# Rows and one-hots of the messages in rings of sets of four, filled in turns of opposite order, and the experts' relu from last part to first

## The chip, the cores and the metric

The kernel runs on one core of a Trainium2 chip. The metric is the device time of one launch in microseconds (us). Before the change it was 1699.68 us, the median of 13 runs (1698.12 to 1706.53). The engines are named PE (matrix products), ACT (activations), DVE (vector operations), POOL (here almost only the issue of indirect DMAs) and SP (issue of the other DMAs). They run side by side and wait for one another by semaphores: each engine posts an increment when an instruction is done, if somebody needs it, and an instruction can wait for a value.

## The reference

One layer of a graph transformer over 6250 nodes of 256 features, with 100000 edges that are sorted by their target:

```
xn = layernorm(x)
h = xn @ W
deg = segment_sum(edge_weight, dst) + 1 ; dinv = rsqrt(deg)
agg = segment_sum(dinv[src]*edge_weight*dinv[dst] * h[src], dst) + dinv^2 * h
gnn = relu(0.5*(layernorm(agg + b)*gamma + beta) + 0.5*xn)
mix = linear attention over xn (8 heads, elu+1 features), projected
x   = x + gnn + mix
z   = layernorm(x)
w, e = softmax over, and places of, the 2 largest of 16 logits z @ gate_w + gate_b
moe = sum over the two experts e of w * (relu(z @ w1[e] + b1[e]) @ w2[e] + b2[e])
x   = x + layernorm(z + moe)*gamma + beta
```

Everything is float32. The edge sum, the gather of h[src] and the segment sum, is the part that the change bears on most; the expert's two products are the other.

## The kernel before

The nodes are held in 49 tiles of 128. The edges are cut into 782 chunks of 128 in the order of their targets. For each chunk, POOL gathers the 128 rows of `h` from memory into a tile `hrow` (line 1364, an indirect DMA of 128 KB), DVE builds a one-hot matrix `hot` of the targets, scaled by the edge weights (line 1369), and PE multiplies the two into a bank `acc` (line 1377; two instructions of 128x256 in the profile for one product). A group of eight chunks shares a bank; DVE then adds it to `agg` (line 1386).

The program is written out by slots, one for each chunk. In slot s stand the gather of chunk s, the one-hots that are due (a product's one-hot is built HOT = 4 slots ahead of it) and the products that are due: chunk c is multiplied in slot c + LAG, with LAG = 11, falling to LAST_LAG = 6 near the end. `hrow` is a pool of ROWS = 22 buffers and `hot` one of HOTS = 9, each taken in turn: gather c needs the place of chunk c - 22, so it waits until that chunk's product is done, and one-hot c waits for product c - 9.

Between these, a planner written out by hand, `Weave`, runs the rest of the layer: pieces are generators that yield the number of slots until their next step. `attend` (lines 573 on) makes keys, queries and their sums for a tile; `residual` (681) joins graph and attention parts; `route` (847) picks the experts; `scatter` (1022) writes the tokens to the experts' slots by indirect DMAs on POOL (line 1040); `expert` (1073) runs one block of 128 slots through an expert; `combine` (1168) gathers the two results of each token on POOL (line 1180) and makes the output. The order of instructions on PE, DVE, ACT and SP is the order in which they are written. 114 expert blocks are run, about one for every seven slots in the middle of the kernel.

`expert` first loads the weights and the tokens through SP, transposes the tokens on PE (`xtp`, copied by ACT), and multiplies by w1 into one bank `hp`, 8 products shown as 16 instructions. Then ACT makes the relu in four parts of 128 columns, f = 0 to 3 (line 1129), each into a part of `hT`, and PE multiplies the four parts by w2 into `yp` (line 1133), again in the order f = 0 to 3:

```
        for f in range(FJ):
            act(hT[:, f, :], hp[:, f, :], AF.Relu, bias=b1[:, f:f + 1], scale=1.0)
        yield apart - lag
        yp = bank("yp")
        for f in range(FJ):
            nc.tensor.matmul(yp[:, :D], hT[:, f, :], w2[:, f, :], start=(f == 0), stop=(f == FJ - 1 and not as_row))
```

After the last chunk, the pool of rows is closed and its room is used for the rows of the combine (`late_row`): NROW places, of which 12 hold shifted tokens ("more") and the others gathered results ("got").

Of the kernel before, what the change touches and what calls it, by code (L numbers as in the profile page):

```python
# [23 lines left out]
F32 = mybir.dt.float32  # L24
# [7 lines left out]
P = 128  # L32
N = 6250
D = 256
# [17 lines left out]
FJ = F // P  # L52
# [4 lines left out]
def rows(t):  # L57
    return min(P, N - t * P)
# [53 lines left out]
HB = 168  # L112
NB3 = 2 * D
QT = 36
ROWS = 22
LAG, LAST_LAG = 11, 6
HOT, HOTS = 4, 9

# [14 lines left out]
def group_of(c):  # L135

    return (c + CPR // 2) // CPR


def product_at(c):  # L140

    return c + max(LAST_LAG, min(LAG, LAST_LAG + (NCH - 30 - c) // 8))


def evicted_at(c):

    return product_at(c) + (3 if c < 16 * PHASES[-2] else 1)
# [111 lines left out]
def windowed_layer(ctx: ExitStack, tc: tile.TileContext, X, ident, loc_t, w_t, src_t, W, b, gamma, beta, wqT, wkvT, wprojT, bproj,  # L259
                   gate_w, gate_b, experts, f_gamma, f_beta, out):  # L260
    nc = tc.nc
# [135 lines left out]
    with tc.tile_pool(name="deg", bufs=1) as sp, \  # L397
# [59 lines left out]
        for n in (C // 2, C // 2, C, C, C):  # L457
# [8 lines left out]
            for c in range(c0, min(c0 + n, NCH)):  # L466
                g0 = 4 * group_of(c)
                h0 = g0
                while h0 < g0 + HI:
                    i = h0 // HB  # L470
# [34 lines left out]
        for i in range(3):  # L505
            v.tensor_reduce(deg16[:, i, :], deg[:, i, :3 * HB].rearrange("p (h s) -> p h s", s=3),
                            axis=AX.X, op=OP.add)
# [37 lines left out]
    mp = msg.enter_context(tc.tile_pool(name="w_msg", bufs=4))  # L545
# [3 lines left out]
    def bank(name):  # L549
        return ps.tile([P, 512], F32, name=name, tag="bank")  # L550
# [103 lines left out]
    def agg(t):  # L654
        return hTs[t // 2][:, t % 2 * D:(t % 2 + 1) * D] if t < 4 else ring[(t - 4) % RING]
# [411 lines left out]
    def sync(to, source):  # L1067
        issued[0] = nc.sync.dma_start(to, source).ins
        return issued[0]
# [3 lines left out]
    def expert(n, j, homes, bank, gap, apart, lag, as_row=False):  # L1073

        def row(i):
            if not loaded.get(i):
                _, regs = nc.values_load_multi_w_load_instructions(
                    s["rows"][0:1, i, j:min(j // 8 * 8 + 8, ends[j])], engines=[mybir.EngineType.SP],
                    min_val=0, max_val=(MOST if i == 0 else NE - 1) * P,
                    skip_runtime_bounds_check_because="bounded by a minimum where it is computed")  # L1080
                loaded[i] = list(regs)
            return loaded[i].pop(0)

        at, slots = row(1), row(0)
        w1p = homes["w1"].take()
        w1 = w1p()
        sync(w1, experts[bass.ds(at, P), :WA])
        w1 = w1.rearrange("p (c f) -> p c f", c=2)
        xp = homes["x"].take()
        xs = xp()  # L1090
        i = sync(xs, xslots[bass.ds(slots, P), :])
        if n is not None:
            for m in range(n + 1, len(PHASES)):
                tc.declare_no_dep(i, group=f"tokens_{m}", reason="a full block takes no more tokens")
            tc.add_to_no_dep_group("loads", i)
        yield gap[0]
        w2p = homes["w2"].take()
        w = w2p()[:, :WROW - WA]
        if as_row:
            sync(w[:, :WB - WA], experts[bass.ds(at, P), WA:WB])  # L1100
            b2 = w[:3, WB - WA:WB - WA + D // 2].bitcast(BF)
            sync(b2, b2rows[bass.ds(at, 3), :])
        else:
            sync(w, experts[bass.ds(at, P), WA:])
            b2 = w[:, WB - WA:]
        w2 = w[:, :FJ * D].rearrange("p (j d) -> p j d", j=FJ)
        b1 = w[:, FJ * D:FJ * D + FJ]
        yield gap[1]
        tp = bank("xtp").rearrange("p (k c) -> p k c", k=4)
        for c in range(2):  # L1110
            nc.tensor.transpose(tp[:, c, :], xs[:, c * P:(c + 1) * P], ident)
        homes["x"].give(xp)
        yield lag
        xTp = homes["xT"].take()
        xT = xTp().rearrange("p (k c) -> p k c", k=2)
        nc.scalar.copy(xT, tp[:, :2, :])  # L1116
        yield apart - lag

        hp = bank("hp").rearrange("p (f c) -> p f c", f=FJ)
        for f in range(FJ):  # L1120
            for c in range(2):
                nc.tensor.matmul(hp[:, f, :], w1[:, c, f * P:(f + 1) * P], xT[:, c, :], start=(c == 0), stop=(c == 1))  # L1122
        homes["xT"].give(xTp)
        homes["w1"].give(w1p)
        yield lag
        hTp = homes["hT"].take()
        hT = hTp().rearrange("p (k c) -> p k c", k=FJ)
        for f in range(FJ):
            act(hT[:, f, :], hp[:, f, :], AF.Relu, bias=b1[:, f:f + 1], scale=1.0)  # L1129
        yield apart - lag  # L1130
        yp = bank("yp")
        for f in range(FJ):
            nc.tensor.matmul(yp[:, :D], hT[:, f, :], w2[:, f, :], start=(f == 0), stop=(f == FJ - 1 and not as_row))  # L1133
        if as_row:
            nc.tensor.matmul(yp[:, :D], ones3, b2, start=False, stop=True)
        homes["hT"].give(hTp)
        yield lag
        y_ = homes["y"].take()
        y = y_()
        if as_row:  # L1140
            nc.scalar.copy(y, yp[:, :D])
        else:
            v.tensor_add(y, yp[:, :D], b2)
        homes["w2"].give(w2p)
        yield 1
        before_it = issued[0]
        i = sync(yslots[bass.ds(slots, P), :], y)
        if n is not None:
            tc.declare_no_dep(i, group="stores", reason="every block has rows of its own", keep=[before_it])
            tc.add_to_no_dep_group("stores", i)  # L1150
            stores[j] = i
            for m, (_, limit) in enumerate(LIMITS):
                if j >= limit:
                    tc.declare_no_dep(i, group=f"gathers_{m}", reason="later blocks hold no token of the first tiles")
                    tc.add_to_no_dep_group(f"late_{m}", i)
        homes["y"].give(y_)
# [85 lines left out]
    def spare(t, n=1):  # L1242
        return range(t, t + n), lambda: Q[:, t:t + n, :].rearrange("p t c -> p (t c)")

    NROW = ROWS
    ringed = ExitStack()
    rp = ringed.enter_context(tc.tile_pool(name="w_ring", bufs=1))
    late = []

    def late_row(i):  # L1250
        if not late:
            late.append(msg.enter_context(tc.tile_pool(name="w_late", bufs=1)).tile([P, NROW, D], F32, name="late"))
        return late[0][:, i, :]
# [11 lines left out]
             "more": Places(*[((), lambda i=i: late_row(i)) for i in range(LATE)], *[spare(t) for t in range(9, 13)]),  # L1265
             "got": Places(*[((), lambda i=i: late_row(i)) for i in range(LATE, NROW)],
                           *[((NT - 1,), lambda j=j: ring[j]) for j in range(RING)])}
# [82 lines left out]
    hrows, hots, accs = {}, {}, {}  # L1350
# [7 lines left out]
    while slot <= evicted_at(NCH - 1) or weave.steps:  # L1358
        for t in range(NT * (slot + PRE) // PRE, NT * (slot + PRE + 1) // PRE if slot < 0 else 0):
            table(t)  # L1360
        c = slot
        if 0 <= c < NCH:
            hrows[c] = rp.tile([P, D], F32, name="hrow", bufs=ROWS)
            nc.gpsimd.indirect_dma_start(  # L1364
                out=hrows[c], out_offset=None, in_=hs,
                in_offset=IndirectOffsetOnAxis(ap=src_t[:, c:c + 1], axis=0))
        for c in hot_at.get(slot, ()):
            hots[c] = mp.tile([P, P], F32, name="hot", bufs=HOTS)
            v.tensor_scalar(hots[c], iota_g[:, group_of(c) % 2, :], loc_t[:, c:c + 1], w_t[:, c:c + 1],  # L1369
                            op0=OP.is_equal, op1=OP.mult)  # L1370
        for c in sum_at.get(slot, ()):
            g = group_of(c)
            begin = c == 0 or group_of(c - 1) != g
            end = c == NCH - 1 or group_of(c + 1) != g
            if begin:
                accs[g] = aps.tile([P, D], F32, name="acc")
            nc.tensor.matmul(accs[g], hots.pop(c), hrows.pop(c), start=begin, stop=end)  # L1377
        for g in evict_at.get(slot, ()):
            acc = accs.pop(g)
            t = (g - 1) // 2  # L1380
            parts = [(t, 0, P)] if g % 2 else [(t, P // 2, P), (t + 1, 0, P // 2)]
            for t, p0, p1 in parts:
                p1 = min(p1, rows(t)) if 0 <= t < NT else 0
                if p1 > p0:
                    assert t in begun and t not in summed, (slot, t, summed_at)
                    v.scalar_tensor_tensor(agg(t)[p0:p1], acc[p0:p1, :], dinv[p0:p1, t:t + 1], agg(t)[p0:p1],  # L1386
                                           op0=OP.mult, op1=OP.add)
        weave.run(slot)
        slot += 1
        if slot == product_at(NCH - 1) + 1:  # L1390
            ringed.close()
# [4 lines left out]
    with tc.If(again[0]), ExitStack() as tail:  # L1396
        tail.enter_context(by_hand(tc))
        mp = tail.enter_context(tc.tile_pool(name="w_again", bufs=2))
# [516 lines left out]
```

## Time and profile before

| What | Value |
|---|---|
| median of 13 runs | 1699.68 us |
| the profiled execution's own time | 1703.65 us |
| its span | 1701.9 us |
| mean granted clock of PE | 0.876 |
| PE busy | 1307.5 us (77%) |
| POOL busy | 955.4 us (56%) |
| DVE busy | 913.4 us (54%) |
| ACT busy | 497.5 us (29%) |
| first gather to last gather | 107.7 to 1400.0 us |

The profile is one execution. A group of instructions is given by line, engine, operation and tile, `out<-in`, with the number of instructions, their busy time and the mean of one in ns, then the idle time that the engine had before them and what ended most of it. "issue" is idle time that ended with nothing that the profile can show; "remote" is a semaphore of another engine whose instruction is not identified. PE's ends are modelled from its starts.

### The profile page before, as it was taken

To read this page: it belongs to the slowest core of one execution; us is meant where nothing else is said; L and a number is where in the kernel's file an instruction comes from. 1 tells how busy PE (TensorE), PEld (TensorE's weight loads), DVE (VectorE), ACT (ScalarE), POOL (GpSimd) and SP (SyncE) were. 2 spreads that over 40 slices of the span, in tenths; PEclk is the share of its full clock that TensorE was granted. 3 is DMA by queue.
4 is the path that set the end of the run, shared out by engine and by line. 5 is a ranking of instruction groups with operands and counts; after the bars stand their busy time and mean duration, and the time that the engine had idled before them with its cause. 6 is when DMAs were issued, how large, how long until landed. Compare 5 with 4: busy or idle time off the path is not lost. (4 is left out here: it accounts for less than half of the span.)

```text
span 1701.9 us, 24398 instructions
## 1 busy us (share of the span) xinstructions
PE 1307.5 (77%) x6927; PEld 1035.0 (61%) x6927; DVE 913.4 (54%) x3303; ACT 497.5 (29%) x1428; POOL 955.4 (56%) x998
## 2 busy tenths in 40 slices
PE   4985988976846778878788787887987998958780
PEld 3853655655634657757566575775766776847660
DVE  7842333346956545644645545555464456626654
ACT  6442333322211122212222122221221132426663
POOL 1036666666666666666665666666666552155531
PEclk9997999988876889979889798998988998978995
DMA  8774555563334557657667565766767785779982
GB/s 271 238 256 136 189 184 164 185 205 95 93 105 142 176 191 235 225 192 232 229 195 256 177 220 191 254 230 193 230 221 235 252 261 179 274 244 312 363 292 72
DMA packets 180593, 357.20 MB, mean 210 GB/s; under 512 B 27157, under 2 KB 119692, under 8 KB 180442
## 3 DMA queue, kind: packets, MB, share of 16 engines
q1 hardware_dynamic: 110334, 204.18, 35.1%
q0 software_dynamic: 47712, 128.17, 24.5%
q10 hardware_dynamic: 22396, 23.10, 4.2%
q8 instruction: 61, 1.00, 0.2%
q14 instruction: 90, 0.74, 0.1%
HBM read 279.28 MB, written 76.06 MB: 209 GB/s over the span
## 5 line engine op out<-in xcount | busy, mean ns | idle before, releaser
L1364 POOL DMA_INDIRECT hrow<-w_hs,src_t x782 | 754.5, 965 | 521.2 <-issue 175.6
L1377 PE MATMUL acc<-hrow,hot 128*128 128x256 f32 x1564 | 452.0, 409 | 41.0 <-issue 25.2
L1377 PEld LDWEIGHTS acc<-hrow,hot 128*128 128x128 f32 x1564 | 294.1, 204 | 115.0 <-issue 64.3
L1369 DVE TENSOR_SCALAR hot<-iota_g,loc_t,w_t 128x128 f32<-128x128 f32 x782 | 245.6, 353 | 127.5 <-PE acc L1377 57.7
L1133 PE MATMUL yp<-early,hT 128*128 128x256 f32 x584 | 167.7, 438 | 57.9 <-issue 44.8
L1129 ACT ACTIVATE hT<-hp,early 128x128 f32<-128x128 f32 x292 | 83.1, 367 | 415.4 <-issue 227.5
L1133 PEld LDWEIGHTS yp<-early,hT 128*128 128x128 f32 x584 | 125.3, 222 | 91.0 <-issue 55.8
L1122 PE MATMUL hp<-Q,early 128*128 128x128 f32 x992 | 131.0, 286 | 11.3 <-ACT Q L1116 6.3
L1122 PEld LDWEIGHTS hp<-Q,early 128*128 128x128 f32 x992 | 127.2, 202 | 17.3 <-ACT Q L1116 7.5
L588 PE MATMUL kq<-early,xnT 128*128 128x512 f32 (+1 forms) x196 | 102.0, 646 | 22.0 <-ACT xnT L584 21.1
L1040 POOL DMA_INDIRECT w_xslots<-Q,slot_i x92 | 90.0, 978 | 45.5 <-issue 41.5
L1133 PE MATMUL yp<-Q,hT 128*128 128x256 f32 x328 | 94.6, 438 | 26.0 <-issue 18.1
L1122 PE MATMUL hp<-Q 128*128 128x128 f32 x832 | 107.5, 285 | 9.1 <-issue 7.5
L1122 PEld LDWEIGHTS hp<-Q 128*128 128x128 f32 x832 | 105.5, 201 | 12.8 <-issue 8.1
L1386 DVE SCALAR_TENSOR_TENSOR agg<-acc,dinv,agg 64x256 f32<-64x256 f32 x135 | 65.1, 482 | 75.7 <-remote 35.4
L749 PE MATMUL mix<-M,two_b 128*128 128x256 f32 (+1 forms) x196 | 66.2, 460 | 48.2 <-issue 31.3
L1133 PEld LDWEIGHTS yp<-Q,hT 128*128 128x128 f32 x328 | 70.1, 222 | 42.1 <-issue 21.2
L1129 ACT ACTIVATE hT<-hp,Q 128x128 f32<-128x128 f32 x164 | 46.7, 370 | 157.4 <-issue 95.7
L1180 POOL DMA_INDIRECT late<-w_yslots,slot_i x48 | 48.1, 1001 | 63.6 <-DVE xn L1208 20.0
L596 DVE SCALAR_TENSOR_TENSOR row<-two_a,two_b 128x256 f32<-128x256 f32 (+1 forms) x49 | 20.8, 425 | 111.9 <-ACT two_b L593 61.7
L749 PEld LDWEIGHTS mix<-M,two_b 128*128 128x128 f32 (+1 forms) x196 | 39.9, 221 | 60.8 <-issue 35.0
L603 PE MATMUL kx<-early,row 128*128 128x257 f32 (+1 forms) x196 | 53.5, 397 | 27.7 <-DVE row L596 26.6
(322 smaller groups left out, 1788.8 us busy)
## 6 DMA issues: line engine op xcount, KB each, us to landing
early<-in_experts SPq DMA_DIRECT2D x60, 642.0 KB
early<-in_experts SPq DMA_DIRECT2D x62, 512.0 KB
Q<-in_experts SPq DMA_DIRECT2D x52, 512.0 KB
Q<-in_experts SPq DMA_DIRECT2D x28, 642.0 KB
w_yslots<-zero_b ACTq DMA_DIRECT2D x16, 1024.0 KB
Q<-w_xslots SPq DMA_DIRECT2D x114, 128.0 KB
w_yslots<-Q SPq DMA_DIRECT2D x114, 128.0 KB
hrow<-w_hs,src_t POOLq DMA_INDIRECT x782
```

Source lines behind the costliest of these rows:

```text
L588: nc.tensor.matmul(kq[:r], xnT[:, k, :r], wkq[:, k, :], start=(k == 0), stop=(k == 1))
L603: nc.tensor.matmul(kx[j][:, :D + 1], kf[:r, j * P:(j + 1) * P], xn[:r], start=(t == 0), stop=(t == NT - 1))
L749: nc.tensor.matmul(mix[:r0, i, :], qT[:, k, i * P:i * P + r0], M[:, k, :], start=(k == 0), stop=False)
L1040: i = nc.gpsimd.indirect_dma_start(out=xslots, out_offset=IndirectOffsetOnAxis(ap=slot_i[:r, t, k:k + 1], axis=0), in_=y[:r], in_offset=No ...
L1122: nc.tensor.matmul(hp[:, f, :], w1[:, c, f * P:(f + 1) * P], xT[:, c, :], start=(c == 0), stop=(c == 1))
L1129: act(hT[:, f, :], hp[:, f, :], AF.Relu, bias=b1[:, f:f + 1], scale=1.0)
L1133: nc.tensor.matmul(yp[:, :D], hT[:, f, :], w2[:, f, :], start=(f == 0), stop=(f == FJ - 1 and not as_row))
L1180: g = nc.gpsimd.indirect_dma_start(out=got[i, k]()[:r], out_offset=None, in_=yslots, in_offset=IndirectOffsetOnAxis(ap=slot_i[:r, t, k:k + ...
L1364: nc.gpsimd.indirect_dma_start(out=hrows[c], out_offset=None, in_=hs, in_offset=IndirectOffsetOnAxis(ap=src_t[:, c:c + 1], axis=0))
L1369: v.tensor_scalar(hots[c], iota_g[:, group_of(c) % 2, :], loc_t[:, c:c + 1], w_t[:, c:c + 1], op0=OP.is_equal, op1=OP.mult)
L1377: nc.tensor.matmul(accs[g], hots.pop(c), hrows.pop(c), start=begin, stop=end)
L1386: v.scalar_tensor_tensor(agg(t)[p0:p1], acc[p0:p1, :], dinv[p0:p1, t:t + 1], agg(t)[p0:p1], op0=OP.mult, op1=OP.add)
```

## The change

The two pools become one tile each, and the program takes their places itself. `in_ring(c, n)` gives chunk c its place in a ring of n: sets of four places follow each other as before, but within a set the order is turned around on every other turn of the ring. So the first chunk of a set takes the place that was filled, and is read, last in that set on the turn before. ROWS falls from 22 to 20, LAG from 11 to 9, HOTS rises from 9 to 12. The gathers carry a token that keeps them in order among themselves on POOL. The relu's parts are made in the order f = 3 to 0, while `yp` still takes them in the order 0 to 3. NROW, the room for late rows, follows the size of the two rings and rises from 22 to 25.

```diff
-ROWS = 22
-LAG, LAST_LAG = 11, 6
-HOT, HOTS = 4, 9
+ROWS, SET = 20, 4
+LAG, LAST_LAG = 9, 6
+HOT, HOTS = 4, 12
...
-        for f in range(FJ):
+        for f in reversed(range(FJ)):
             act(hT[:, f, :], hp[:, f, :], AF.Relu, bias=b1[:, f:f + 1], scale=1.0)
...
-    NROW = ROWS
+    NROW = ROWS + HOTS * P // D - 1
     ringed = ExitStack()
     rp = ringed.enter_context(tc.tile_pool(name="w_ring", bufs=1))
+    hrow_ring = rp.tile([P, ROWS, D], F32, name="hrow")
+    hot_ring = rp.tile([P, HOTS, P], F32, name="hot")
+
+    def in_ring(c, n):
+
+        i, turn = c % SET, c // n % 2
+        return c % n - i + (SET - 1 - i if turn else i)
...
-            hrows[c] = rp.tile([P, D], F32, name="hrow", bufs=ROWS)
-            nc.gpsimd.indirect_dma_start(
+            hrows[c] = hrow_ring[:, in_ring(c, ROWS), :]
+            tc.stamp_issue_order_token(nc.gpsimd.indirect_dma_start(
                 out=hrows[c], out_offset=None, in_=hs,
-                in_offset=IndirectOffsetOnAxis(ap=src_t[:, c:c + 1], axis=0))
+                in_offset=IndirectOffsetOnAxis(ap=src_t[:, c:c + 1], axis=0)).ins, "rows")
...
-            hots[c] = mp.tile([P, P], F32, name="hot", bufs=HOTS)
+            hots[c] = hot_ring[:, in_ring(c, HOTS), :]
```

## The prediction

> **What bounds the kernel now.** I read the page first, then busy time by stretches, the list of waits, and the timeline at two places.
>
> ```profile
> PE 1307.5 (77%) x6927; PEld 1035.0 (61%) x6927; DVE 913.4 (54%) x3303; ACT 497.5 (29%) x1428; POOL 955.4 (56%) x998
> L1364 POOL DMA_INDIRECT hrow<-w_hs,src_t x782 | 754.5, 965 | 521.2 <-issue 175.6
> L1377 PE MATMUL acc<-hrow,hot 128*128 128x256 f32 x1564 | 452.0, 409 | 41.0 <-issue 25.2
> L1133 PE MATMUL yp<-early,hT 128*128 128x256 f32 x584 | 167.7, 438 | 57.9 <-issue 44.8
> L1129 ACT ACTIVATE hT<-hp,early 128x128 f32<-128x128 f32 x292 | 83.1, 367 | 415.4 <-issue 227.5
> ```
>
> PE is the busiest engine but not full; POOL's gathers come next, with 521 us of idle time between them. By stretches of 100 us (length; then busy us and instructions of PE, PEld, DVE, ACT, POOL; granted clock, DMA share, GB/s):
>
> ```profile
> 500.00:600.00 100.00, 61.45 (x260) 47.69 (x260) 49.21 (x194) 12.64 (x34) 64.17 (x66) 0.72 0.48 155
> 700.00:800.00 100.00, 80.15 (x403) 65.16 (x402) 52.43 (x196) 20.52 (x60) 64.03 (x68) 0.88 0.64 211
> 1300.00:1400.00 100.00, 88.83 (x494) 76.41 (x493) 45.69 (x143) 23.46 (x74) 59.59 (x62) 0.95 0.80 263
> ```
>
> From 600 to 1300 us, PE stands idle for 130.5 of 700 us (the seven stretches add up to 569.5 busy). In the list of waits (us in total, times, longest):
>
> ```profile
> ACT hT L1129 <- issue: 323.2, 42, 17.0
> POOL hrow L1364 <- PE acc L1377: 111.7, 100, 4.0
> PE yp L1133 <- issue: 62.8, 30, 4.6
> DVE hot L1369 <- PE acc L1377: 57.7, 25, 5.8
> PE yp L1133 <- ACT hT L1129: 20.5, 6, 6.3
> ```
>
> Everybody waits for somebody: POOL for products, PE's second expert product for the relu, the relu for "issue", which is nothing the profile shows. The timeline shows what that is. Between 118 and 149 us (start, us, engine, what):
>
> ```profile
> 119.94 1.88 PE L588 MATMUL kq<-early,xnT 128*128 128x512 f32 x4
> 125.79 1.56 PE L1377 MATMUL acc<-hrow,hot 128*128 128x256 f32 x6
> 141.69 0.95 POOL L1364 DMA_INDIRECT hrow<-w_hs,src_t  x1 [0.30 <-issue]
> 146.68 0.60 ACT L592 ACTIVATE two_a<-kq 128x512 f32<-128x512 f32 x1 [22.77 <-remote]
> 148.28 1.23 PE L603 MATMUL kx<-early,row 128*128 128x257 f32 x2 [20.93 <-DVE row L596]
> ```
>
> The kq that ACT reads at 146.68 was finished at 121.8. ACT learnt of it 25 us later, after POOL's run of 28 gathers had stopped at a full ring. The semaphore records of PE say the same: one at 126.3, one at 134.7, one at 138.9, then six within a microsecond from 146.6. So **while POOL issues gathers back to back, PE's completions reach the others late, and most of them in a burst after POOL pauses**. The ordinary cycle of the middle is the same thing in small:
>
> ```profile
> 797.14 1.95 PE L1122 MATMUL hp<-Q,early 128*128 128x128 f32 x16
> 799.90 0.95 POOL L1364 DMA_INDIRECT hrow<-w_hs,src_t  x1 [0.30 <-issue]
> 802.10 1.14 ACT L1129 ACTIVATE hT<-hp,early 128x128 f32<-128x128 f32 x4 [7.99 <-PE acc L1377]
> 802.33 0.94 POOL L1364 DMA_INDIRECT hrow<-w_hs,src_t  x1 [1.48 <-PE acc L1377]
> 802.52 0.70 PE L1133 MATMUL yp<-early,hT 128*128 128x256 f32 x2 [0.61 <-issue]
> ```
>
> hp is done at 799.1; the relu starts at 802.10, in the burst that also frees POOL, and only then does yp follow. POOL runs seven gathers (8.75 us at a pitch of 0.95 + 0.30), pauses 1.75 us, and again: 10.5 us for one expert and seven chunks. PE's own work in it is 7 x 452.0/782 = 4.05 for products, 238.5/114 = 2.09 for hp (131.0 + 107.5 us over 114 blocks) and 262.3/114 = 2.30 for yp, 8.4 in all.
>
> **The change part by part.** Counts come from the two built programs. The sum is made against the profiled execution, 1703.65 us, 4 us above the median of 1699.68.
>
> *Rings.* Since turns are filled in opposite order, the first chunk of a set takes the place that was read last, and its wait covers the other three. Gathers that wait for PE fall from 760 to 191, one-hots that wait for it from 365 to 62, and POOL's separate semaphore instructions from 908 to 336. On POOL this is worth nothing directly: the pitch is 1.25 us for gathers without any wait (109 to 117 us), with one and with two. But matmuls that nobody waits for post nothing: PE's semaphore updates fall from 2314 to 1815 (products 782 to 458, yp 445 to 277). In the middle PE posts 773 in 700 us, 11.6 in a cycle of 10.5; in runs of seven gathers 4.1 of them (mean of 24 runs) arrive during the run, so that 7.5 wait for the pause. With 1815/2314 of them it is 9.1, and 5.0 wait: a third less. If PE's idle time there shrinks with the backlog, a third of 130.5 us goes: **-43**. Bounds: 0, if the updates are held until POOL pauses however few they are; -117, if nothing is held and POOL's 8.75 us set the cycle (1.75 x 67 cycles). I take the third because some updates do come through during a run, so that the number of them matters.
>
> *Fewer rows, LAG 9.* POOL now stops 17 to 20 chunks ahead of the products instead of 22, 18.5 in the mean. Where PE hangs until POOL's ring is full (127 to 146, and 386 to 395 us), that comes 3.5 x 1.25 = 4.4 us sooner: **-9**, between 0 and -13 (a third such place about 540). Rows are not short: products waited 41.0 us in all, and LAG shifts products and all that follows by two slots together. The scatters' groups on POOL move 2 to 4 gathers forward with them, which I cost at nothing: the cover is the run-ahead of 17; without it one group of eight costs 8 x 1.28 us, once each.
>
> *Relu from the last part.* Parts 3, 2, 1, 0: yp starts with part 0, so with the last relu. Four relus take 1.14 us; yp now starts 0.42 after the first (802.52 - 802.10), then about 1.14 + 0.05: +0.77 wherever PE waits for the relu. PE waited before yp 30 + 6 times: up to +28. Of waits that remain, some end in a burst where PE has slack against POOL's run; half, **+14**, ends 0 and +28. The other side: between 1514 and 1523 us, yp's matmuls go one by one with gaps of 1.3, 2.4 and 2.2, as single updates of ACT arrive; one wait instead of four takes perhaps 4 of these 6 us: **-4** (0 to -6). A matmul with a wait has the same pitch as one without, so the 324 waits removed from PE are worth nothing else.
>
> *Tokens and late places.* The gathers stood in order already; nothing. Three more places for the combine's rows bear on the tail, where POOL's combine gathers wait 20.0 us for DVE: 0 to -5, taken as 0.
>
> Sum: -43 - 9 + 14 - 4 = -42: 1661.6 for this execution, **1658** against the median.
>
> *A rule against a row.* The Trainium skill, "TensorE: Matmul & The Clock Gate", section "The cost: per-tile semaphore tail", says that increments of matmuls serialize at about 26 ns each. By that alone the 499 dropped updates would be at most 13 us. The burst at 802.0 has them 45 ns apart, which would be 22; what the trace shows at 122 us is a delay a thousand times that, so I go by the row. "DMA: Bandwidth & Descriptors", section "Rules for kernel authors", speaks against the change: issue a transfer early and wait late; here run-ahead is cut, and by that rule rows would get scarcer. The 41.0 us before products say that they are not the shortage.
>
> **Rivals.**
>
> *POOL stops at every fourth gather, on the other side.* The hold ends only when POOL pauses, and its runs are now 4 or 8 instead of 7. Three cycles of 8 x 1.25 + 1.75 = 11.75 and one of four gathers, in which PE's 8.4 decide: 43.65 us for four experts instead of 42.0. Over 67 cycles +28; with -9, +14 and -4 it is +29: 1729. It decides as soon as the backlog at the pause does not shrink. For it: bursts come 1.1 to 1.8 us after POOL's last gather almost without exception. Against it: a run of four is over before most of the holding.
>
> *The hold vanishes.* If the 9.1 updates fit into what gets through, the cycle is POOL's, some 9.0 us: -1.5 x 67 = -100, with relu and rows about 1600. For it: from 109 to 117 us, where gathers waited for nothing, updates came at once. Against: from 118 to 135 us no gather waited for PE either, and the updates were late already.
>
> *Relu on the path, nothing else moves.* +28 - 9 = +19: 1719. For it: 36 waits before yp. Against: the burst that starts the relu starts POOL too.
>
> *The updates do not matter.* The waits removed were all long satisfied and the cycle stays at 10.5 us: within 5 us of 1700.
>
> **How the numbers follow.** Chances: forecast 0.42, stop at every fourth 0.27, hold vanishes 0.13, relu 0.08, nothing 0.10. The likeliest gives 1658, and by itself 1630 to 1685 (its first term between -70 and -15). To leave out no more than 2 in 10 the range reaches from the vanished hold's edge, 1595, to the fourth-gather rival with relu's upper half, 1732. Within 0.2% (3.4 us, about what a measurement can tell): half of the last, 0.05. Faster: 0.42 + 0.13 + 0.03 = 0.58; slower: 0.27 + 0.08 + 0.02 = 0.37.
>
> **What would show it.** Right: PE busy 84 to 88 of 100 us from 600 to 1300, fewer waits of ACT's hT on "issue" (323.2 us), DVE's wait for acc (57.7) nearly gone, the hang at 127 us shorter than 20.9. Relu: yp about 1.2 us after the first relu in the middle. Wrong: POOL in runs of exactly 4 or 8 with PE's busy share at or below 80, relus still starting in bursts 3 us after hp. The weakest step is that idle time shrinks with the backlog: the cause of the hold is not known.

## The result, and the profile after

The changed kernel took 1722.8 us, the median of 13 runs (1716.45 to 1734.41); the kernel before 1701.46 us over 59 runs. The ratio is 1.0128, 95% interval 1.0115 to 1.0140: **slower by 21 us**, where 42 us faster was forecast. It lies inside the range, on the other side, 6 us from the rival "POOL stops at every fourth gather" (1729) and 4 us from "relu on the path" (1719).

The page of the changed kernel has these lines in place of those shown of before:

```profile
PE 1299.9 (76%) x6927; PEld 1037.1 (60%) x6927; DVE 909.2 (53%) x3303; ACT 498.5 (29%) x1428; POOL 956.3 (56%) x998
L1372 POOL DMA_INDIRECT hrow<-w_hs,src_t x782 | 755.0, 966 | 531.0 <-issue 204.7
L1385 PE MATMUL acc<-hrow,hot 128*128 128x256 f32 x1564 | 441.8, 402 | 44.9 <-issue 33.1
L1377 DVE TENSOR_SCALAR hot<-iota_g,loc_t,w_t 128x128 f32<-128x128 f32 x782 | 243.6, 353 | 22.3 <-remote 17.2
L1133 PE MATMUL yp<-early,hT 128*128 128x256 f32 x584 | 173.2, 448 | 94.6 <-ACT hT L1129 73.1
L1394 DVE SCALAR_TENSOR_TENSOR agg<-acc,dinv,agg 64x256 f32<-64x256 f32 x135 | 65.1, 482 | 134.3 <-remote 83.1
```

The page of the kernel before has, for DVE:

```profile
L1369 DVE TENSOR_SCALAR hot<-iota_g,loc_t,w_t 128x128 f32<-128x128 f32 x782 | 245.6, 353 | 127.5 <-PE acc L1377 57.7
L1386 DVE SCALAR_TENSOR_TENSOR agg<-acc,dinv,agg 64x256 f32<-64x256 f32 x135 | 65.1, 482 | 75.7 <-remote 35.4
```

The engines do the same work in nearly the same time; what grew is waiting. The idle time before the one-hots fell from 127.5 to 22.3 us, as the fewer waits let expect, but that before DVE's addition to `agg` rose from 75.7 to 134.3: a part of DVE's waiting moved from the one-hot to a later step. The idle time before the larger group of yp (that of `early`) rose from 57.9 to 94.6. Busy time by stretches, in the same columns as before:

```profile
500.00:600.00 100.00, 63.19 (x262) 48.65 (x262) 51.83 (x205) 15.33 (x42) 64.53 (x68) 0.71 0.50 163
700.00:800.00 100.00, 79.81 (x399) 66.53 (x398) 52.12 (x194) 20.45 (x60) 61.51 (x64) 0.87 0.63 205
1300.00:1400.00 100.00, 88.10 (x481) 76.49 (x480) 45.75 (x141) 22.88 (x72) 57.23 (x61) 0.93 0.77 255
```

Over 600 to 1300 us PE was to rise to 84 or more of 100. The two answers for the whole stretch, of before and of after, one line each:

```profile
600.00:1300.00 700.00, 569.48 (x2866) 463.82 (x2867) 377.95 (x1420) 151.11 (x443) 449.31 (x467) 0.88 0.66 216
```

```profile
600.00:1300.00 700.00, 549.91 (x2821) 455.23 (x2821) 367.45 (x1395) 146.50 (x429) 442.81 (x462) 0.88 0.65 213
```

PE's idle time went from 130.5 to 150.1 us there, +19.6 instead of -43. Not all of it is lost time, since the same window holds less work: POOL has 462 instructions in it instead of 467, at 1.5 us each a loss of 7.5 us. Over the whole kernel the last gather starts 14.6 us later (at 1414.6 instead of 1400.0 us), and what follows it takes 304.6 us instead of 301.9: of the 17.3 us between the two profiled spans, most arises among the gathers. In the list of waits of the changed kernel (total, times, longest):

```profile
ACT hT L1129 <- issue: 340.7, 43, 20.6
PE yp L1133 <- ACT hT L1129: 105.8, 32, 10.1
POOL hrow L1372 <- PE acc L1385: 83.4, 41, 5.0
PE yp L1133 <- issue: 39.5, 13, 12.1
DVE hot L1377 <- PE acc L1385: 3.2, 3, 1.3
```

The relu still waits for "issue" (340.7 us against 323.2), and PE waits before yp for 145.3 us in these two rows against 83.3. The timeline of the changed kernel shows the hold in its longest form, from 935 to 967 us:

```profile
936.06 1.14 ACT L1129 ACTIVATE hT<-hp,early 128x128 f32<-128x128 f32 x4 [7.30 <-issue]
937.25 1.99 PE L1133 MATMUL yp<-early,hT 128*128 128x256 f32 x8 [1.00 <-ACT hT L1129]
939.51 1.95 PE L1122 MATMUL hp<-Q 128*128 128x128 f32 x16
957.71 1.14 ACT L1129 ACTIVATE hT<-hp,Q 128x128 f32<-128x128 f32 x4 [19.76 <-issue]
959.56 1.00 POOL L1372 DMA_INDIRECT hrow<-w_hs,src_t  x1 [3.23 <-remote]
959.86 2.07 PE L749 MATMUL mix<-M,two_b 128*128 128x256 f32 x4 [9.40 <-ACT two_b L706]
```

hp is done at 941.5. The relu begins at 957.7, after POOL's 16 indirect DMAs (eight gathers and eight scatters) from 936.3 to 956.3 without a break. In the first two lines the relu's turned order is seen: yp starts 1.19 us after the first relu, where it was 0.42.

I grouped POOL's indirect DMAs between 600 and 1300 us by runs without a gap, and took the time from each run's start to the next one's, and PE's busy share in it, from the trace's records:

| kernel | length of run | runs | mean us to the next run | us for one DMA | PE's share |
|---|---|---|---|---|---|
| before | 7 | 33 | 10.49 | 1.50 | 0.85 |
| before | 14 and 15 | 4 | 21.5 | 1.45 | 0.62 |
| after | 4 | 31 | 6.49 | 1.62 | 0.95 |
| after | 8 | 27 | 11.97 | 1.50 | 0.80 |
| after | 16 | 6 | 23.31 | 1.46 | 0.55 |

Nearly every run of the changed kernel is 4, 8 or 16 long. The short ones cost: 31 x 4 DMAs at 1.62 instead of 1.50 us are 15 us. The kernel before had short runs too, seven of a single DMA with 2.24 us to the next among them, so that over the whole stretch the difference is smaller: 700/467 = 1.499 against 700/462 = 1.515 us for one DMA. In a run of four PE is busy nearly throughout, so I take it that POOL waits for PE there; in the long ones PE waits for POOL to stop.

### The profile page after: what moved, and what is told of

Its sections match the earlier page's. It is cut to its first block, busy times and chain, and to the rows that moved or that the text cites. A ratio compares the mean times of both kernels' runs of the same rounds, so it can differ in the third digit from the quotient of the medians.

```text
span 1719.2 us, 23794 instructions
## 1 busy us (share of the span) xinstructions
PE 1299.9 (76%) x6927; PEld 1037.1 (60%) x6927; DVE 909.2 (53%) x3303; ACT 498.5 (29%) x1428; POOL 956.3 (56%) x998
## 5 line engine op out<-in xcount | busy, mean ns | idle before, releaser
L1385 PE MATMUL acc<-hrow,hot 128*128 128x256 f32 x1564 | 441.8, 402 | 44.9 <-issue 33.1
L1385 PEld LDWEIGHTS acc<-hrow,hot 128*128 128x128 f32 x1564 | 289.9, 201 | 109.1 <-issue 63.0
L1377 DVE TENSOR_SCALAR hot<-iota_g,loc_t,w_t 128x128 f32<-128x128 f32 x782 | 243.6, 353 | 22.3 <-remote 17.2
L1133 PE MATMUL yp<-early,hT 128*128 128x256 f32 x584 | 173.2, 448 | 94.6 <-ACT hT L1129 73.1
L1394 DVE SCALAR_TENSOR_TENSOR agg<-acc,dinv,agg 64x256 f32<-64x256 f32 x135 | 65.1, 482 | 134.3 <-remote 83.1
L1122 PE MATMUL hp<-Q 128*128 128x128 f32 x848 | 113.9, 292 | 7.4 <-ACT Q L1116 4.1
L1122 PEld LDWEIGHTS hp<-Q 128*128 128x128 f32 x848 | 111.7, 208 | 11.6 <-ACT Q L1116 4.7
L1180 POOL DMA_INDIRECT late<-w_yslots,slot_i x58 | 58.3, 1005 | 62.2 <-issue 14.7
L588 PEld LDWEIGHTS kq<-early,xnT 128*128 128x128 f32 (+1 forms) x196 | 39.3, 206 | 72.2 <-issue 36.8
L740 DVE TENSOR_TENSOR h<-hp,bias_b 128x512 f32<-128x512 f32 (+1 forms) x25 | 17.0, 678 | 107.0 <-remote 87.6
L734 PE MATMUL hp<-w_sb,two_a 128*128 128x256 f32 (+1 forms) x196 | 58.0, 448 | 14.9 <-ACT two_a L706 8.7
```

The source lines that it names most:

```text
L588: nc.tensor.matmul(kq[:r], xnT[:, k, :r], wkq[:, k, :], start=(k == 0), stop=(k == 1))
L734: nc.tensor.matmul(hp[:r0, i, :], agT[:, k, i * P:i * P + r0], w_sb[:, k, :], start=(k == 0), stop=(k == 1))
L1180: g = nc.gpsimd.indirect_dma_start(out=got[i, k]()[:r], out_offset=None, in_=yslots, in_offset=IndirectOffsetOnAxis(ap=slot_i[:r, t, k:k + ...
```

## The experiments

The theories: **A**, the sets of four cost, since POOL may stop only at every fourth chunk; **B**, the reversed relu costs; **C**, two rows less and LAG 9 cost. Every kernel was timed beside the kernel before, on the same chip, within one session. A ratio is given with its 95% interval; it is an estimate of its own and can differ a little from the quotient of the two medians beside it.

**Something else came first.** In the first session the kernel before took 1469.85 us, not 1701. The sessions are of two kinds: in some, before takes 1466 to 1470 us, in the others 1687 to 1701, with the same program; two of the chips were met in both kinds, so it is not a property of a chip. I call the second kind *held*: there PE's completions come late while POOL issues its gathers, as in the profile that the prediction was made from. What makes a session held is not known and could not be set, so some kernels were run more than once.

### The relu alone

```diff
 (before)
-        for f in range(FJ):
+        for f in reversed(range(FJ)):
             act(hT[:, f, :], ...
```

> The kernel before with the relu's four parts made last to first, nothing else. Theory A (the sets of four in the ring of rows are what costs): the relu is mostly hidden, +0 to +8 us. Theory B (the relu is what costs; PE now waits for the last part): most of the loss, +14 to +28 us, and PE's idle time before yp grows by as much. Theory C (20 rows and LAG 9 cost, whatever the order of places): +0 to +8 us.

> The reversed relu alone again, in search of a chip on which completions are held up (the kernel before at some 1700 us). There, Theory A (sets of four) expects 0 to +8 us, Theory B (relu) +14 to +28 us. Where before takes some 1470 us, both expect the 0 to +4 us measured already.

Not held: 1471.34 against 1469.85, ratio 1.0013 (0.9997 to 1.0030). Held: 1698.74 against 1700.71, **1.0002 (0.9987 to 1.0017)**. B falls as a cause by itself, though PE's waits before yp did grow in the held profile, from 83.3 us in 36 waits to 98.4 in 53:

```profile
PE yp L1133 <- ACT hT L1129: 71.9, 36, 10.3
PE yp L1133 <- issue: 26.5, 17, 3.5
```

The 15 us more at yp are not in the total. A likely reason, which no run tests, is that the burst that starts the relu also starts POOL's next run, so that PE has that run's length to catch up.

### The rings with the relu forward

```diff
 (after)
-        for f in reversed(range(FJ)):
+        for f in range(FJ):
             act(hT[:, f, :], ...
```

> The changed kernel with the relu in its old order 0 to 3. Theory A (sets of four): still +13 to +25 us. Theory B (relu): within 7 us of before. Theory C (20 rows, LAG 9): still +13 to +25 us.

> The changed kernel with the relu forward again, beside the one above. With completions held up, Theory A (sets of four) expects +13 to +25 us, Theory B (relu) within 7 us. Otherwise 0 to +4 us as measured.

Not held: 1.0014 (0.9998 to 1.0031). Held: 1712.63 against 1700.71, **1.0062 (1.0043 to 1.0081)**, +11 us: a little below A's span, above B's. The runs are those of the changed kernel (27 of four, 30 of eight, 6 of sixteen). So the rings cost by themselves, and turning the relu adds some 10 us beside them though it costs nothing alone (the 1.0128 and the 1.0062 come from different sessions, with the kernel before at 1701.46 and 1700.71). Why it does stays open: the waits before yp are 142.9 us here and 145.3 in the changed kernel.

### The rings in plain order

```diff
 (after)
-        return c % n - i + (SET - 1 - i if turn else i)
+        return c % n
```

> The changed kernel with the places of both rings taken in the same order on every turn, so that each gather and each one-hot waits for its own predecessor again; 20 rows, LAG 9, 12 one-hots and the reversed relu stay. Theory A (sets of four): POOL's runs are no longer multiples of four, PE busy from 600 to 1300 us returns to 81 of 100, and the loss falls to 0 to +8 us. Theory B (relu): +14 us or more remains. Theory C (20 rows, LAG 9): +14 us or more remains.

> The changed kernel with both rings filled in the same order on every turn, the reversed relu kept, where completions are held up. Theory A (sets of four): every gather may stop again, the relu alone was worth -2 to +3 us, so -3 to +6 us, and POOL's runs are no longer multiples of four. Theory C (sizes): +12 us or more. If the reversed relu costs only beside fewer waits, this run keeps below +8 us as well. Where before takes some 1470 us: 0 to +5 us as measured.

> The changed kernel with both rings in the same order on every turn, reversed relu kept, where completions are held up. Theory A (sets of four): -3 to +6 us. Theory C (sizes): +12 us or more. Otherwise 0 to +3 us as measured twice.

Not held: 1.0018 (0.9998 to 1.0038) and 1.0010 (0.9996 to 1.0024). Held: 1693.25 against 1686.79, **1.0020 (0.9998 to 1.0041)**. With the same sizes, the same tokens and the same reversed relu, taking the places in the same order on every turn leaves little of the loss; the commonest run is seven long again (27 of them). This speaks for A. The changed kernel itself was not timed beside it, so the 1.0020 is set beside a 1.0128 from sessions in which before took 1701 us.

### The sizes alone

```diff
 (before)
-ROWS = 22
-LAG, LAST_LAG = 11, 6
-HOT, HOTS = 4, 9
+ROWS = 20
+LAG, LAST_LAG = 9, 6
+HOT, HOTS = 4, 12
```

> The kernel before with ROWS 20, LAG 9 and HOTS 12, its pools and the relu as before. Theory A (sets of four): within 8 us of before. Theory B (relu): within 5 us of before. Theory C (20 rows, LAG 9): +13 to +25 us.

> ROWS 20, LAG 9, HOTS 12 in the old pools again, hoped for where completions are held up (before at some 1700 us). There, Theory A (the sets of four cost: POOL may stop only at every fourth chunk) expects -5 to +4 us; Theory C (two rows less and LAG 9 cost) expects +8 to +14 us, all of the +11 that the rings cost with the relu forward. Where before takes some 1470 us: 0 to +4 us as measured.

> ROWS 20, LAG 9, HOTS 12 in the old pools, still sought where completions are held up. There, Theory A (sets of four) -5 to +4 us; Theory C (sizes) +8 to +14 us. Otherwise 0 us as measured twice.

Not held: 1.0015 (1.0001 to 1.0028) and 0.9992 (0.9973 to 1.0010). Held: 1686.26 against 1686.79, **0.9991 (0.9967 to 1.0014)**: at most 2.4 us of loss. C falls.

### The changed kernel where nothing is held

> The changed kernel itself, once more, because the four parts ran on a chip on which the kernel before takes 1470 us and PE's completions are not held up during POOL's gathers. Theory H (the loss exists only where completions are held up): on such a chip the change is within 5 us of before; on a chip where before takes some 1700 us it is +13 to +28 us again. Theory N (the change costs by itself, held up or not): +13 us or more on either.

1468.1 against 1466.41 us, ratio **1.0007 (0.9989 to 1.0024)**: the change that costs 21 us in a held session costs nothing here. Its page, a stretch, and a part of its timeline:

```profile
L1372 POOL DMA_INDIRECT hrow<-w_hs,src_t x782 | 755.2, 966 | 325.6 <-issue 205.4
L1133 PE MATMUL yp<-early,hT 128*128 128x256 f32 x584 | 149.9, 403 | 0.8 <-ACT hT L1129 0.8
```

```profile
700.00:800.00 100.00, 88.80 (x502) 76.95 (x500) 66.08 (x252) 28.96 (x83) 75.93 (x80) 0.95 0.80 268
```

```profile
804.84 1.95 PE L1122 MATMUL hp<-Q 128*128 128x128 f32 x16
806.12 0.95 POOL L1372 DMA_INDIRECT hrow<-w_hs,src_t  x1 [0.30 <-PE hp L1122]
806.87 1.14 ACT L1129 ACTIVATE hT<-hp,Q 128x128 f32<-128x128 f32 x4 [7.72 <-PE hp L1122]
```

The relu starts 0.08 us after hp (804.84 + 1.95), while POOL goes on without a break: 80 DMAs in 100 us, 1.25 us each. The idle time before yp is 0.8 us instead of 94.6. POOL's pitch is the bound: 782 gathers at 1.25 us and 92 scatters at 1.28 are 1095 us, and the gathers take 1096 us from first to last (108.4 to 1204.0). Neither the order of places nor that of the relu matters to it. Theory H holds, N falls.

### Rows or one-hots

```diff
 (after, one run with the first line, one with the second)
-            hots[c] = hot_ring[:, in_ring(c, HOTS), :]
+            hots[c] = hot_ring[:, c % HOTS, :]
...
-            hrows[c] = hrow_ring[:, in_ring(c, ROWS), :]
+            hrows[c] = hrow_ring[:, c % ROWS, :]
```

> The changed kernel with only the rows in turns of opposite order; the one-hots take their places in the same order on every turn. Where completions are held up: Theory A1 (POOL's stops at every fourth row cost) +14 to +22 us and runs of 4, 8, 16; Theory A2 (the one-hots' sets cost) -2 to +6 us. Otherwise 0 to +4 us.

> The changed kernel with only the one-hots in turns of opposite order; the rows in the same order on every turn. Where completions are held up: Theory A1 (rows) -2 to +6 us; Theory A2 (one-hots) +14 us or more. Otherwise 0 to +4 us.

Both held. Rows alone in sets: 1701.86 against 1688.69, **1.0061 (1.0026 to 1.0097)**, with 31 runs of four, 27 of eight and 5 of sixteen. One-hots alone: 1693.92, **1.0035 (1.0004 to 1.0066)**, with 27 runs of seven. The rows cost, but less than A1 expected, and beside plain order (1.0020) the one-hots are not told from nothing. The gathers from the 300th to the last took 820 us with rows in sets and 805 with one-hots in sets, 804 in plain order. The parts do not add up to 1.0128: the changed kernel itself was timed in sessions in which before took 1701 us, these in sessions with 1687 to 1689, and it was not run in one of these.

### A breath on POOL

```diff
 (before; the gathers carry the order token, as do the memsets)
+    breath = rp.tile([16, 256], mybir.dt.uint8, name="breath")
...
+            if c % 4 == 3:
+                for _ in range(4):
+                    tc.stamp_issue_order_token(nc.gpsimd.memset(breath, 0).ins, "rows")
```

> The kernel before, with four short memsets on POOL after every fourth gather, some 1 us in all, so that POOL issues no DMA for that long. Theory P (completions get through whenever POOL's issue of gathers pauses for a microsecond): where they are held up, PE busy from 600 to 1300 us rises to 84 or more of 100 and the time falls by 30 to 100 us, in spite of 195 us of added work on POOL, which has 520 us of idle time. Theory Q (they get through only when POOL is idle, or for another reason): the time rises by 20 to 150 us. Where before takes some 1470 us, POOL sets the pace, and both expect +150 to +220 us.

> The kernel before with 1.4 us of memsets on POOL after every fourth gather, sought where completions are held up. Theory P (it is the issue of DMAs that holds completions; a pause of 1.4 us lets them through): below the 1753 us measured where nothing is held up, or within 10 us of it, with no relu later than 2 us after hp while POOL is at its gathers. Theory Q (POOL at work holds them, whatever the work): 1780 us or more. Otherwise 1753 us as measured.

Not held: 1753.42 us, 1.1958 (1.1934 to 1.1983), above the 150 to 220 us that both theories expected; the memsets lengthen POOL's pitch, which is the bound. Held: 1788.52 us, 1.0599 (1.0517 to 1.0681; two runs). By its total the second run meets Q, and P's numbers were missed. But the stretch from 600 to 1300 us, where the breaths are, is the same in both, not held first, held second:

```profile
600.00:1300.00 700.00, 537.18 (x2656) 433.15 (x2655) 349.17 (x1276) 139.01 (x402) 537.32 (x820) 0.87 0.61 201
```

```profile
600.00:1300.00 700.00, 537.95 (x2638) 437.03 (x2637) 344.19 (x1264) 139.75 (x401) 537.22 (x819) 0.86 0.61 201
```

and the held session's timeline has places such as this one, where the relu follows hp at once:

```profile
805.29 1.52 POOL L1370 MEMSET breath<- 16x256 uint8 x4
806.28 1.95 PE L1122 MATMUL hp<-Q 128*128 128x128 f32 x16
808.32 1.14 ACT L1129 ACTIVATE hT<-hp,early 128x128 f32<-128x128 f32 x4 [7.01 <-issue]
```

hp is done at 808.23 and the relu starts at 808.32. The last gather starts at 1500 us where nothing is held and at 1503 where it is; without breaths the kernel before differed by 220 us between these two sessions (1688.69 and 1468.29). The 35 us that remain arise after the last gather, where POOL issues the gathers of the combine without breaths. How late the relu is can be read from the records of every expert block: from the end of hp's last matmul to the start of the first relu, between 600 and 1300 us.

| kernel | session | blocks | median us | later than 2 us | longest us |
|---|---|---|---|---|---|
| before | held | 67 | 3.84 | 50 | 16.1 |
| after | held | 65 | 1.48 | 31 | 18.7 |
| after | not held | 92 | 0.09 | 1 | 4.5 |
| breath | held | 57 | 0.21 | 7 | 6.8 |
| breath | not held | 57 | 0.09 | 0 | 0.1 |

The seven late relus of the held breath run miss P's condition, but they tell more than the median does. POOL's scatters have no breaths, so a group of eight scatters with the gathers beside it makes a run of twelve DMAs without a break; six of the seven start within such a run or within 0.6 us of its end, and the seventh, 2.1 us late, starts in a breath. So a break of 1.4 us after every fourth gather, filled with other work of POOL, removes most of the hold, and it stays where the breaks are missing: **the cause is POOL's issue of DMAs without a break**, not POOL being at work, and not the number of completions, which is that of the kernel before. The changed kernel's typical relu is sooner than before, but its long runs hold it longer, up to 18.7 us.

### Shorter breaths, and fewer rows

```diff
 (the breath above, short)
-                for _ in range(4):
+                for _ in range(1):
...
 (the breath above, every eighth)
-            if c % 4 == 3:
-                for _ in range(4):
+            if c % 8 == 7:
+                for _ in range(2):
...
 (sizes alone, above, with fewer rows)
-ROWS = 20
+ROWS = 14
```

> The kernel before with one memset on POOL after every fourth gather (0.31 us and some 0.1 us of gaps), 80 us of added work on POOL. Theory P (it is the unbroken issue of gathers that holds completions, and a short break is enough): where they are held up, -40 to -110 us, relus within 1 us of hp, PE busy 86 or more of 100 from 600 to 1300. Theory P2 (a break must be as long as the 1.2 us in which the burst comes): -10 to +40 us. Where nothing is held up: +60 to +90 us.

> The same added work on POOL in half as many breaks: two memsets after every eighth gather. Theory P: where completions are held up, less gained than with a break after every fourth, -20 to -80 us, because the hold grows within a run of eight. Theory P2: as much or more than with the short one, as the break is twice as long. Where nothing is held up: +60 to +90 us.

> The kernel before with ROWS 14, LAG 9, HOTS 12: POOL's ring is full eight gathers sooner. Theory P: where completions are held up, POOL stops sooner, the hangs are shorter, -5 to -40 us. Theory C (rows become scarce): +5 to +40 us. Where nothing is held up: within 5 us.

The session was not held: 1498.46 against 1467.05 us for one memset after every fourth gather, 1.0211 (1.0150 to 1.0272); 1535.38 for two after every eighth, 1.0463 (1.0405 to 1.0520); 1467.32 with 14 rows, 1.0007 (0.9993 to 1.0021). The first costs 31 us, half of the least expected, the second 68, although both add the same number of memsets; why is open. Eight rows of run-ahead are not needed where nothing is held. Whether the short breath gains where completions are held stays open; it was not measured there. None of these kernels is faster than the kernel before, beyond its interval, in either kind of session.

## Why the prediction was wrong

*What was right.* The hold was read rightly: completions late while POOL issues, in a burst after it pauses. The one-hots' waits went (57.7 to 3.2 us in the row for acc). Yp starts 1.19 us after the first relu. The first hang came sooner to its end:

```profile
136.78 0.95 POOL L1372 DMA_INDIRECT hrow<-w_hs,src_t  x1 [0.30 <-issue]
141.57 0.37 ACT L584 COPY xnT<-tp 128x256 f32<-128x256 f32 x1 [15.60 <-remote]
142.00 3.78 PE L588 MATMUL kq<-early,xnT 128*128 128x512 f32 x4 [12.74 <-ACT xnT L584]
```

POOL's first run is 24 gathers instead of 28, PE hangs for 12.7 us instead of 20.9; PE was busy for 80.64 of the 100 us from 100 to 200, before 74.30. POOL stops 4.9 us sooner (136.78 against 141.69), where 4.4 us was forecast for each such place. But it was given back: between 300 and 400 us PE was busy for 72.72 against 76.73. The sizes alone measured 0.9991 (0.9967 to 1.0014), so of the *-9* at most 6 us can have reached the total.

*The step that failed* is the first term, -43: "If PE's idle time there shrinks with the backlog, a third of 130.5 us goes". The backlog did shrink, and the idle time did not follow. In the trace's records of PE's semaphore the updates between 600 and 1300 us fell from 773 to 503. What waited for a pause, counted from the end of a run's last DMA to the start of the next run, fell from 7.9 updates after a run of seven to 6.7 after a run of eight and 3.2 after one of four (33, 27 and 31 runs). Yet PE's idle time grew from 130.5 to 150.1 us. During a run fewer got through, too: 4.9 in a run of seven before, 3.1 in a run of eight and 3.0 in one of sixteen after. What is held comes when POOL's issue breaks, not when the number of updates is small; the breath run, which posts as many as the kernel before, shows it from the other side. The bound 0, "if the updates are held until POOL pauses however few they are", was much nearer the truth, and I took the middle. (The prediction's 773 is a count of records and too low for what PE posts: the trace has 1924 records for 2314 updates of the kernel before and 1516 for 1815 of the changed one; the instructions that post in this stretch are 939 and 611.)

*The rival that came nearest* is "POOL stops at every fourth gather". Its runs of 4 and 8 came, and its total, 1729, is 6 us off. Its condition, that the backlog at the pause does not shrink, did not hold as it was worded (7.9 to 6.7 and 3.2). Its working was only half right: runs of eight cost 1.50 us per DMA, what runs of seven cost, and those of four 6.49 us rather than 8.4, but there were as many of four as of eight, where I had one of four to three of eight. That its total is so near is in part luck, since its -9 and +14 did not come out so either.

*The relu's term*, +14 on the path: alone it measured 0 (0.9987 to 1.0017), beside the rings some +10 (1.0128 against 1.0062). The sum had one term for both cases, and what makes the difference is open. *The -4* for yp with single waits, and the 0 for the tail, no run tells from nothing.

*A wider gap, though not what made the sum miss*, was to read one profile as the kernel's. Where nothing is held, PE stands idle for 60.9 us from 600 to 1100 us (439.10 busy, in the changed kernel) against 94.9 in the kernel before where it is held, POOL is the bound, and the change moved the time by 0.07%.

*The page on TensorE* that was weighed (the Trainium skill, "TensorE: Matmul & The Clock Gate", "The cost: per-tile semaphore tail") gave, by an estimate from its 26 ns, at most 13 us for the dropped increments. No run here can show or refute it: in the session without a hold the rings with the relu forward measured 1.0014 (0.9998 to 1.0031), but there POOL is the bound, so that a little time saved on PE would not be seen. The rule on issuing early ("DMA: Bandwidth & Descriptors", "Rules for kernel authors") is not visible here either: where nothing is held, 14 rows did as well as 22, 1.0007 (0.9993 to 1.0021).

## What to carry to other kernels

A wait that is taken off an engine is not worth its count. Ask instead where that engine may now stop: here the removed waits were points at which POOL could pause, and most completions came in such pauses. And time a change in more than one session before explaining it: the same two programs differed by 1.3% in one and by nothing in another.

## What was not expected of the hardware

- The same program takes 1466 to 1470 us in some sessions and 1687 to 1701 in others, two of the chips being met in both. In the longer ones PE's completions come late while POOL issues indirect DMAs back to back: in the kernel before, ACT's relu starts at the median 3.84 us and at most 16.1 us after hp, and in the first hang an activation began 25 us after the matmul that it reads had ended (121.8 to 146.68). In the shorter ones the median is 0.09 us, at the same pitch of 1.25 us.
- A break of 1.4 us after every fourth gather, spent on memsets of 0.31 us, removes most of this: the last gather starts at 1503 us instead of 1500 in the other kind of session, and the median relu 0.21 us after hp. Runs of twelve DMAs without a break still held it up to 6.8 us.
- In the held sessions the trace also has fewer records of PE's semaphore than PE posts: 1924 for 2314 in the kernel before and 1824 for 2314 with breaths, where the breath run without a hold has 2316. Why is open.
- One indirect gather costs POOL 0.95 + 0.30 us whether its instruction waits for nothing, for one or for two semaphores: 572 separate semaphore instructions less on POOL moved the session without a hold by 0.0007 (-0.0011 to 0.0024).
